# Normalising a softmax: sums and reciprocals moved through DRAM instead of through TensorE products

## The chip, the cores and the metric

The kernel runs on one core of a Trainium2 chip. The time is device microseconds of one launch, and the time before is the median of three runs, 3791.74 us (3791.0 to 3793.28). A profile of one execution stands beside it; its span is 3780.8 us.

The engines are called PE (TensorE), ACT (ScalarE), DVE (VectorE), POOL (GpSimd) and SP (SyncE, which issues nearly all transfers here). PEld is PE's weight load, which runs beside its products.

## The reference

Four layers follow one another on x of shape (4, 128, 64, 64): four images b, 128 channels, N = 4096 positions.

- Layer 0 is self-attention over positions: energy = q^T k with 16-dimensional q and k, `softmax(energy, axis=-1)`, out = v attn^T, and then `gamma * out + x`.
- Layer 1 is two 3x3 convolutions with quantised weights and activations, batch norm and a residual.
- Layer 2 is a selective scan (Mamba): projections, a recurrence h = dA * h + dBx over the 4096 positions for 256 inner channels and 16 states, an output product, a group norm, silu and a residual.
- Layer 3 is self-attention again, with 64-dimensional q, k and v, an output product wo, and a residual.

What matters here is the softmax of layers 0 and 3. For each of the 4096 output positions the kernel needs the sum of 4096 exponentials, and the 128 channels of that position are divided by it.

## The kernel before, in words

**Stages.** There are eight attention stages in the order of the list `stages`: layer 0 of images 0, 1 and 2, then layer 3 of image 0, layer 0 of image 3, and layer 3 of images 1, 2 and 3. An attention stage goes over 16 blocks of CB = 256 output positions, and each block over four quarters of the 4096 keys. A quarter (index t) is eight energy products (L491), two exponentials of 128x1024 on ACT (L507), the products with v (L544), and the products with a block of ones (L554) that give the sums. The products with v and the sums of a block gather in one PSUM tile `us` of 128 x 2 x 256: half 0 holds the channels, half 1 the sums. The sums arrive as four partial sums, each laid on 32 partitions in turn (partitions 0, 32, 64 and 96 carry one each), because the keys are split over four row groups of PE.

**The end of a block pair (`parts` and `finish`).** After each block ACT evicts both halves (L580, in layer 0 times gamma, and L582). Two blocks make 512 columns, index c of 8. For these `finish` runs. Its first four products (L601) with the column `sel4` (ones at partitions 0, 32, 64, 96) add the four partial sums and turn the 512 sums into columns, 128 x 4. DVE takes their reciprocals (L610). Four more products (L614), with each reciprocal column spread as weights against the identity, lay the reciprocals along rows, the same on all 128 partitions. DVE multiplies (L622). In layer 0 the result is added to x in the padded image `xpad` (L627). In layer 3 it goes through the output product (L633) and the residual addition (L637) and is stored (L640).

**Beside it** run the convolutions (`convolutions`), the preparation of the scan (`preparation`), and the scan. The scan goes over 512 steps m (4 images x 8 column blocks x 16 states). A step is, on DVE, the product of ud with the first half of a broadcast tile `bc` (L981), the readout of the step before with the second half of its tile (L971), and two recurrences (L989). ACT computes the decays `da` (L954) and copies the last column (L964); POOL adds up the readouts (L1006). Each `bc` tile is a 512 KB broadcast load from DRAM (L941) with three buffers, so the load for step m waits for the readout of step m-3.

**Order.** Nothing reorders at run time. The class `Order` plans all engines: each chain of work is a generator that yields `op(engine, time, needs)`, with its estimated time; `lag` is the estimated time after which a transfer's data has landed. The chain with the smallest estimated start plus 0.15 us times its rank is placed next. `finish` has rank 0, the scans rank 3. The result is one fixed list of instructions on each engine. One PSUM bank (`gtile`) is shared by the convolutions, the scan's products and `finish`; `bank=True` asks for it and `release` gives it back. `port=True` marks DVE work that the planner keeps apart from POOL's. SP is one such list too: a transfer that waits holds up those behind it.

The heart of the old `finish`:

```python
nc.tensor.matmul(sc[:, k : k + 1], lhsT=ss[:, k * P : (k + 1) * P], rhs=sel4, ...)
...
nc.vector.reciprocal(r, sc[:, 0:4])
...
nc.tensor.matmul(sc[:, k * P : (k + 1) * P],
                 lhsT=r[:, k : k + 1].to_broadcast([P, P]), rhs=ident, ...)
...
nc.vector.tensor_mul(us, us, sc)
```

Of the kernel before, what the change touches and what calls it, by code (L numbers as in the profile page):

```python
# [8 lines left out]
F32 = mybir.dt.float32  # L9
# [6 lines left out]
AF = mybir.ActivationFunctionType  # L16
ALU = mybir.AluOpType
AX = mybir.AxisListType
PSUM = bass.MemoryType.PSUM

P = 128
W = 64
N = W * W
TB = 512
NTB = N // TB
# [11 lines left out]
CB = 256  # L37
# [8 lines left out]
class Order:  # L46
# [16 lines left out]
    @staticmethod  # L63
    def op(engine, time, *needs, bank=False, table=None, port=False, lag=0.0):
        return engine, time, needs, bank, table, port or engine == "POOL", lag
# [6 lines left out]
    def mark(self, *key):  # L72
        self.marks[key] = self.end

    def release(self):
        self.bank = self.end[0]
# [36 lines left out]
def img(ap):  # L113
    return ap.rearrange("p (a b) -> p a b", b=W)


def inner(t, c):
    return t[:, 1 + c * ROWS : 1 + (c + 1) * ROWS, 1 : 1 + W]
# [14 lines left out]
def conv_seq_kernel(ctx: ExitStack, tc: tile.TileContext, i: dict, out: bass.AP):  # L133
    nc = tc.nc
    B = out.shape[0]

    const = ctx.enter_context(tc.tile_pool(name="const", bufs=1))
    sml = ctx.enter_context(tc.tile_pool(name="sml", bufs=2))
    dram = ctx.enter_context(tc.tile_pool(name="dram", bufs=2, space=bass.MemoryType.DRAM))
# [3 lines left out]
    att = fast.enter_context(tc.tile_pool(name="att", bufs=2))  # L143
# [6 lines left out]
    def gtile(name):  # L150
        return ps_g.tile([P, TB], F32, tag="g", name=name)
# [14 lines left out]
    for c in range(NTB // 2):  # L166
# [3 lines left out]
            out=staged[0, c],  # L170
            in_=i["x"][0].rearrange("c (k r) w -> c k (r w)", r=ROWS)[:, 2 * c : 2 * c + 2],
# [3 lines left out]
    ident = const.tile([P, P], F32, tag="ident", name="ident")  # L175
# [44 lines left out]
    for key, d, t in (("i", 2 * D0, bq0r), ("j", D0, bk0r)):  # L220
        low = [const.tile([P, 1], F32, tag=k + key, name=k + key) for k in ("low_", "lowb_")]
        r = ident.rearrange("p (a k b) -> p k a b", k=2, b=d)
# [5 lines left out]
    gam0 = const.tile([P, 1], F32, tag="gam0", name="gam0")  # L228
    nc.scalar.dma_start(out=gam0, in_=i["L0_conv_gamma"].unsqueeze(0).to_broadcast([P, 1]))
    gbv0 = const.tile([P, 1], F32, tag="gbv0", name="gbv0")  # L230
    nc.vector.tensor_mul(gbv0, gam0, bv0)

    sel4 = const.tile([P, 1], F32, tag="sel4", name="sel4")
    nc.gpsimd.memset(sel4, 0.0)
    for k in range(4):
        nc.gpsimd.memset(sel4[32 * k : 32 * k + 1, :], 1.0)

    def rsqrt(r, var):

# [98 lines left out]
    order = Order()  # L338
    op, mark, release = order.op, order.mark, order.release
# [18 lines left out]
    NQ = NJ // 8  # L358
    NS = NCB * NQ
    its, jts, vts, es, ps, uss = {}, {}, {}, {}, {}, {}  # L360
# [204 lines left out]
    def parts():  # L565


        for s, (layer, b) in enumerate(stages):
            for c in range(NTB):
                k0 = s * NCB + 2 * c  # L570
                us = ss = None
                for k in range(k0, k0 + 2):
                    need = [("parts", s * NTB + c - 2)] if s or c > 1 else []
                    yield op("ACT", 0.45, ("sums", (k + 1) * NQ - 1), *need)
                    if us is None:
                        us = att.tile([P, TB], F32, tag="us", name="us", bufs=2)
                        ss = att.tile([P, TB], F32, tag="ss", name="ss", bufs=2)
                    cols = slice((k - k0) * CB, (k - k0 + 1) * CB)
                    scale = gam0 if layer == 0 else 1.0
                    nc.scalar.activation(us[:, cols], uss[k][:, 0, :], AF.Copy, scale=scale)  # L580
                    yield op("ACT", 0.4)
                    nc.scalar.copy(ss[:, cols], uss.pop(k)[:, 1, :])  # L582
                    mark("evict", k)
                if layer == 3:
                    order.add(1, residual(b, c))
                order.add(0, finish(s, c, us, ss))

    def residual(b, c):
        n = NTB * b + c
        yield op("SP", 0.1, *([("out", n - 1)] if n else []), lag=2.5)  # L590
        outs[b, c] = o = att.tile([P, TB], F32, tag="o", name="o", bufs=1)
        nc.sync.dma_start(out=o, in_=x2s[b][c])
        mark("res", n)

    def finish(s, c, us, ss):
        layer, b = stages[s]
        n = 2 * NTB * b + (0 if layer == 0 else NTB) + c
        yield op("PE", 0.65, bank=True)
        sc = gtile("sc")
        for k in range(4):  # L600
            nc.tensor.matmul(  # L601
                sc[:, k : k + 1],
                lhsT=ss[:, k * P : (k + 1) * P],
                rhs=sel4,
                start=True,
                stop=True,
            )
        yield op("DVE", 0.18)
        r = rall[:, 4 * n : 4 * n + 4]
        nc.vector.reciprocal(r, sc[:, 0:4])  # L610

        yield op("PE", 1.15)
        for k in range(4):
            nc.tensor.matmul(  # L614
                sc[:, k * P : (k + 1) * P],
                lhsT=r[:, k : k + 1].to_broadcast([P, P]),
                rhs=ident,
                start=True,
                stop=True,
            )  # L620
        yield op("DVE", 0.69)
        nc.vector.tensor_mul(us, us, sc)  # L622
        release()
        if layer == 0:
            yield op("DVE", 0.75, ("x", b, c), port=True)
            xi = inner(xpad, c)
            nc.vector.scalar_tensor_tensor(xi, img(us), gbv0, xi, ALU.add, ALU.add)  # L627
            mark("xi", b, c)
            mark("parts", s * NTB + c)
        else:  # L630
            yield op("PE", 1.06, bank=True)
            g = gtile("o3")
            nc.tensor.matmul(g, lhsT=wo3, rhs=us, start=True, stop=True)  # L633
            mark("parts", s * NTB + c)
            yield op("DVE", 0.69, ("res", NTB * b + c))
            o = outs.pop((b, c))
            nc.vector.tensor_add(o, g, o)  # L637
            release()
            yield op("SP", 0.1, lag=2.5)
            nc.sync.dma_start(  # L640
                out=out[b].rearrange("c h w -> c (h w)")[:, c * TB : (c + 1) * TB], in_=o
            )
            mark("out", NTB * b + c)
# [369 lines left out]
    with tc.manual_schedule():  # L1013
        for rank, chain in (
            (1, parts()),
            (1, convolutions()),
            (1, preparation()),
            (1, output()),
            (1, lasts()),
            (3, energies()),  # L1020
            (4, exponentials()),
            (4, products()),
            (3, decays(0)),
            (3, decays(1)),
            (3, scans()),
            (3, additions()),
            (3, fetches()),
            (3, images()),
        ):
            order.add(rank, chain)  # L1030
        order.run()
# [9 lines left out]
    g = gtile("ok_t")  # L1041
# [470 lines left out]
```

## Time and profile before

| engine | busy us | share of the span | costliest lines |
|---|---|---|---|
| PE | 3462.1 | 92% | L544 1537.2, L491 530.2 + 195.5, L554 544.1 |
| DVE | 2963.8 | 78% | L989 1102.9 + 150.3, L971 669.2, L981 656.6 |
| ACT | 2512.8 | 66% | L507 1002.4, L954 702.0 |
| POOL | 1316.0 | 35% | L1006 1216.6 |

The groups of the change: L601 73.1 us and L614 73.2 us of PE (512 records each), L610 11.5 us and L622 43.8 us of DVE (64 each), L580 30.2 + 24.5 us and L582 46.8 us of ACT (128 each in all).

A share of the whole span mixes stages that have different limits. The page's row of 40 slices, each 94.5 us long, shows busy tenths per slice and tells the stages apart. A list of waits says, for each pair of lines, how long an engine sat idle until the other line ended, how often, and the longest such wait; "issue" means that nothing in the profile was waited for. A DMA row gives the number of transfers, the size of each and the median time from issue to landing. SPq in a timeline is SP issuing a transfer.

### The profile page before, as it was taken

How to read it: one execution, taken by the hardware profiler on the slowest of the kernel's cores; microseconds unless marked ns; L12 is line 12 of the kernel's file. 1: busy time of each engine (PE TensorE's matmuls, PEld its weight loads, DVE VectorE, ACT ScalarE, POOL GpSimd, SP SyncE). 2: the span in 40 equal slices, each digit the busy share in tenths (PEclk: the TensorE clock that was granted, in tenths of full speed). 3: DMA queues.
4: the chain of work that ended last, by engine and by line, in shares of the span. 5: the costliest groups of instructions: out<-in, count | busy, mean ns of one | idle time of the engine just before them, and what ended most of it. 6: DMA issues, size and time to landing. Idle time of an engine off the chain costs nothing.

```text
span 3780.8 us, 72475 instructions
## 1 busy us (share of the span) xinstructions
PE 3462.1 (92%) x30839; PEld 2258.3 (60%) x30839; DVE 2963.8 (78%) x2824; ACT 2512.8 (66%) x3658; POOL 1316.0 (35%) x568
## 2 busy tenths in 40 slices
PE   5999988999989999889998999999898988999998
PEld 3766656666656666645555666665454555556665
DVE  2039999999989999999998999989998888960000
ACT  2357767777776767677777777776776677764443
POOL 0004434444424444434443443443444444430000
PEclk8999999999999999999999999999999999999999
DMA  2013333333433333433443333333433433331000
GB/s 69 1 38 95 92 110 99 86 97 93 111 100 91 93 91 98 116 93 95 109 121 109 97 90 80 96 106 86 120 99 97 123 92 104 102 89 36 15 13 16
DMA packets 203662, 327.92 MB, mean 87 GB/s; under 512 B 50608, under 2 KB 53440, under 8 KB 203328
## 3 DMA queue, kind: packets, MB, share of 16 engines
q1 hardware_dynamic: 196384, 322.09, 31.8%
q8 instruction: 243, 3.98, 0.4%
q10 hardware_dynamic: 6944, 1.10, 0.2%
q14 instruction: 91, 0.75, 0.1%
HBM read 304.27 MB, written 18.87 MB: 85 GB/s over the span
## 4 chain that ended last, share of the span: by engine, by line
PE 60%; DVE 23%; ACT 11%; issue 5%; DMA 2%; ACTq 0%; DVEq 0%; SPq 0%
PE us L544 24%; PE e L491 13%; DVE hs L989 9%; PE us L554 8%; DVE hs L981 4%; DVE hs L971 3%; ACT da L954 2%; ACT p L507 2%; PE conv L649 2%; PE xh L738 2%; PE sc L614 1%; PE proj L462 1%; PE proj L420 1%; PE yo L868 1%; PE sc L601 1%
## 5 line engine op out<-in xcount | busy, mean ns | idle before, releaser
L1006 POOL TENSOR_TENSOR y<-y,hs 128x1024 f32<-128x1024 f32 x512 | 1216.6, 2376 | 2050.1 <-DVE hs L971 2022.7
L544 PE MATMUL us<-p,v 128*32 128x256 f32 (+1 forms) x12288 | 1537.2, 390 | 125.0 <-ACT p L507 125.0
L544 PEld LDWEIGHTS us<-p,v 128*32 128x32 f32 (+1 forms) x12288 | 1009.6, 138 | 564.8 <-issue 171.6
L507 ACT ACTIVATE p<-e 128x1024 f32<-128x1024 f32 x1024 | 1002.4, 1019 | 430.3 <-PE e L491 258.5
L989 DVE TENSOR_TENSOR_SCAN hs<-da,hlast,hs 128x512 f32<-128x512 f32 x896 | 1102.9, 1264 | 40.8 <-ACT da L954 40.5
L954 ACT ACTIVATE da<-dt,amat 128x512 f32<-128x512 f32 x1024 | 702.0, 691 | 271.1 <-DVE hs L989 263.7
L971 DVE TENSOR_TENSOR hs<-hs,bc 128x1024 f32<-128x1024 f32 x512 | 669.2, 1307 | 40.1 <-ACT hlast L964 39.6
L981 DVE TENSOR_TENSOR hs<-ud,bc 128x1024 f32<-128x1024 f32 x512 | 656.6, 1282 | 0.2
L554 PE MATMUL us<-p,ones 128*32 128x256 f32 x8192 | 544.1, 383 | 0.0
L491 PE MATMUL e<-it,v 64*128 64x256 f32 x4096 | 530.2, 398 | 14.0 <-ACT p L507 12.5
L491 PEld LDWEIGHTS e<-it,v 64*128 64x128 f32 x4096 | 382.2, 191 | 162.2 <-issue 89.7
L610 DVE RECIPROCAL rall<-sc 128x4 f32<-128x4 f32 x64 | 11.5, 179 | 529.2 <-PE sc L601 529.2
L554 PEld LDWEIGHTS us<-p,ones 128*32 128x32 f32 x8192 | 236.6, 110 | 209.1 <-issue 67.7
L491 PEld LDWEIGHTS e<-it,j 64*128 64x128 f32 x2048 | 140.9, 189 | 102.9 <-issue 69.5
L491 PE MATMUL e<-it,j 64*128 64x256 f32 x2048 | 195.5, 309 | 6.9 <-ACT p L507 5.9
L964 ACT COPY hlast<-hs 128x2 f32<-128x2 f32 x448 | 85.6, 191 | 130.8 <-DVE hs L989 125.0
L989 DVE TENSOR_TENSOR_SCAN hs<-da,hs 128x512 f32<-128x512 f32 x128 | 150.3, 1206 | 1.8 <-ACT da L954 1.7
L738 PEld LDWEIGHTS <-w 128*128 128x128 bf16 x576 | 51.7, 98 | 106.5 <-issue 58.4
L738 PE MATMUL xh<-x,w 128*128 128x512 fp8e4 x384 | 94.6, 383 | 3.8 <-DVE x L709 2.8
L1010 POOL TENSOR_TENSOR y<-y,sz 128x1024 f32<-128x1024 f32 x32 | 95.8, 2995 | 2.5
L601 PEld LDWEIGHTS sc<-sel,ss 128*128 128x128 f32 x512 | 65.0, 190 | 40.2 <-issue 18.3
L601 PE MATMUL sc<-sel,ss 128*128 128x1 f32 x512 | 73.1, 254 | 14.5 <-ACT ss L582 10.4
(158 smaller groups left out, 2517.9 us busy)
## 6 DMA issues: line engine op xcount, KB each, us to landing
bc<-bc_d SPq DMA_DIRECT2D x512, 512.0 KB, 4.8
x_in<-in_x SPq DMA_DIRECT2D x16, 512.0 KB, 4.7
xpad<-in_x SPq DMA_DIRECT2D x32, 256.0 KB, 3.2
x_d<-yo SPq DMA_DIRECT2D x32, 256.0 KB, 2.5
x_in<-x_d SPq DMA_DIRECT2D x16, 512.0 KB, 6.1
o<-x_d SPq DMA_DIRECT2D x32, 256.0 KB, 5.3
out<-o SPq DMA_DIRECT2D x32, 256.0 KB, 2.7
bc_d<-xd SPq DMA_DIRECT2D x64, 32.0 KB, 1.7
```

The costliest lines, as they stand in the source:

```text
L491: nc.tensor.matmul(e[k % 4 // 2][:, k % 2, k // 4, :], lhsT=jts[s][row : row + D3, col : col + P], rhs=its[s][row : row + D3, c * CB : (c ...
L507: nc.scalar.activation(p, es[t][h], AF.Exp)
L544: nc.tensor.matmul(us[rows, 0, :], lhsT=vts[s][:, 8 * q + k, cols], rhs=ps[t, h][:, k % 2, k // 4, :], start=False, stop=False,)
L554: nc.tensor.matmul(us[32 * m : 32 * m + 32, 1, :], lhsT=ones[:, 0:32], rhs=ps[t, m // 2][:, k % 2, k // 4, :], start=False, stop=q == NQ - ...
L601: nc.tensor.matmul(sc[:, k : k + 1], lhsT=ss[:, k * P : (k + 1) * P], rhs=sel4, start=True, stop=True,)
L738: nc.tensor.matmul(g, lhsT=w3[:, k // len(rhs), lhs[k % len(rhs)] : lhs[k % len(rhs)] + P], rhs=x[:, rhs[k % len(rhs)]], start=(k == 0), s ...
L954: nc.scalar.activation(da, live["in", g][0][:, h, :], AF.Exp, scale=amat[:, h, n : n + 1])
L971: nc.vector.tensor_mul(hs, hs, bcs.pop(m)[:, 1:2, :].to_broadcast([P, 2, TB]))
L981: nc.vector.tensor_mul(hs, ud, bcs[m][:, 0:1, :].to_broadcast([P, 2, TB]))
L989: nc.vector.tensor_tensor_scan(hs[:, h, :], das.pop((m, h)), hs[:, h, :], hlast[:, n, h : h + 1] if g % NTB else 0.0, ALU.mult, ALU.add,)
L1006: nc.gpsimd.tensor_tensor(y, y, hss.pop(m), ALU.add)
L1010: nc.gpsimd.tensor_tensor(y, y, live.pop(("sz", g)), ALU.mult)
```

## The change

The eight products of `finish` are replaced by transfers. The four rows of partial sums (partitions 0, 32, 64, 96 of half 1 of `us`) are written to DRAM (`s_d`, 4 x 512). They are read back as `st`, 128 x 4 x 4, so that a partition holds four sums in four parts each. DVE adds the parts (`tensor_reduce`) and takes the reciprocals. These are written to DRAM (`r_d`, 512) and read back as `rb`, the same row on all 128 partitions. DVE multiplies by `rb` from SBUF, with gamma in the same instruction in layer 0. The two halves of a PSUM block are evicted by one copy instead of two, and `sel4` goes. The aim is to take this work off PE, the busiest engine.

```diff
-                    nc.scalar.activation(us[:, cols], uss[k][:, 0, :], AF.Copy, scale=scale)
-                    yield op("ACT", 0.4)
-                    nc.scalar.copy(ss[:, cols], uss.pop(k)[:, 1, :])
+                        us = att.tile([P, 2, 2, CB], F32, tag="us", name="us", bufs=2)
+                    nc.scalar.copy(us[:, :, k - k0, :], uss.pop(k))
...
-        yield op("PE", 0.65, bank=True)
-        sc = gtile("sc")
-        for k in range(4):
-            nc.tensor.matmul(
-                sc[:, k : k + 1],
-                lhsT=ss[:, k * P : (k + 1) * P],
-                rhs=sel4,
...
-        yield op("DVE", 0.18)
+        yield op("SP", 0.1, lag=2.2)
+        s_d = dram.tile([4, TB], F32, tag="s_d", name="s_d")
+        nc.sync.dma_start(out=s_d, in_=us[0:P:32, 1, :])
+        us = us[:, 0, :]
+        mark("s_d", k)
+        yield op("SP", 0.1, ("s_d", k), lag=2.5)
+        st = att.tile([P, 4, 4], F32, tag="st", name="st", bufs=2)
+        nc.sync.dma_start(out=st, in_=s_d.rearrange("g (p e) -> p g e", e=4))
+        mark("st", k)
+        yield op("DVE", 0.3, ("st", k))
         r = rall[:, 4 * n : 4 * n + 4]
-        nc.vector.reciprocal(r, sc[:, 0:4])
-
-        yield op("PE", 1.15)
-        for k in range(4):
-            nc.tensor.matmul(
-                sc[:, k * P : (k + 1) * P],
-                lhsT=r[:, k : k + 1].to_broadcast([P, P]),
-                rhs=ident,
...
-        yield op("DVE", 0.69)
-        nc.vector.tensor_mul(us, us, sc)
-        release()
+        nc.vector.tensor_reduce(r, st.rearrange("p g e -> p e g"), AX.X, ALU.add)
+        nc.vector.reciprocal(r, r)
+        yield op("SP", 0.1, lag=2.2)
+        r_d = dram.tile([TB], F32, tag="r_d", name="r_d")
+        nc.sync.dma_start(out=r_d.rearrange("(p e) -> p e", e=4), in_=r)
+        mark("r_d", k)
+        yield op("SP", 0.1, ("r_d", k), *([("mul", k - 1)] if k else []), lag=3.0)
+        rb = att.tile([P, TB], F32, tag="rb", name="rb", bufs=1)
+        nc.sync.dma_start(out=rb, in_=r_d.unsqueeze(0).to_broadcast([P, TB]))
+        mark("rb", k)
+        yield op("DVE", 0.75, ("rb", k), port=True)
+        scale = gam0 if layer == 0 else 1.0
+        nc.vector.scalar_tensor_tensor(us, us, scale, rb, ALU.mult, ALU.mult)
+        mark("mul", k)
```

## The prediction, made before the changed kernel had run

> **What bounds the kernel now.** First the page's slices of the span, to see which engine is full when:
>
> ```profile
> PE   5999988999989999889998999999898988999998
> DVE  2039999999989999999998999989998888960000
> ```
>
> There are three stages. Slices 1 to 3 are TensorE alone (attention of image 0 in layer 0). From slice 4 to 35 both rows stand at 8 or 9. After that DVE has nothing left and TensorE works through layer 3 of the last image. Next, busy time by stage (stretch, its length, then busy us and instructions of PE, weight loads, DVE, ACT, POOL, then clock and DMA):
>
> ```profile
> 252.00:3366.00 3114.00, 2859.93 (x24358) 1863.74 (x24360) 2902.04 (x2667) 2245.85 (x3342) 1308.95 (x543) 0.97 0.37 99
> 3500.00:3600.00 100.00, 99.45 (x1328) 62.44 (x1324) 3.12 (x6) 41.56 (x50) 0.00 (x0) 1.00 0.04 12
> ```
>
> 252 to 3366 us is the stretch of the scans. DVE is busy for 93.2% of it, PE for 91.8%: two engines share the bound, DVE slightly ahead. In the tail PE is at 99%. So PE time saved counts fully in the tail, and in the scan stretch only where it shortens a DVE wait. What DVE waits for, 300 to 3366 us:
>
> ```profile
> DVE rall L610 <- PE sc L601: 59.6, 37, 3.3
> DVE hs L989 <- ACT da L954: 42.2, 33, 6.9
> DVE hs L971 <- ACT hlast L964: 39.6, 39, 2.6
> DVE us L622 <- PE sc L614: 16.2, 23, 2.9
> ```
>
> L610 and L622 are the two waits which the change removes: 75.8 us. DVE never waits for the loads of bc. Now the end of the scan stretch, in the timeline of the SP queue and of the rest:
>
> ```profile
> 3386.95 5.42 SPq L932 DMA_DIRECT2D x_d<-yo  x8
> 3417.27 3.51 SPq L375 DMA_DIRECT2D x_in<-x_d  x4
> ```
>
> The last image is stored by 3392.4, plus 2.5 us to landing (the page's x_d row): 3394.9. Its load is issued only at 3417.3, when PE has finished image 2 and freed the p buffers. PE therefore enters the tail 22.4 us late. One block's end in the tail:
>
> ```profile
> 3730.94 1.05 PE L601 MATMUL sc<-sel,ss 128*128 128x1 f32 x8
> 3732.27 1.16 PE L614 MATMUL sc<-ident,rall 128*128 128x128 f32 x8 [0.28 <-DVE rall L610]
> 3733.36 2.00 PE L491 MATMUL e<-it,v 64*128 64x256 f32 x16
> ```
>
> From the first sum product to the next energies PE spends 3733.36 - 3730.94 = 2.42 us. Last, the landing times, page and two narrow windows of the DMA view:
>
> ```profile
> bc<-bc_d SPq DMA_DIRECT2D x512, 512.0 KB, 4.8
> xpad<-in_x SPq DMA_DIRECT2D x32, 256.0 KB, 3.2
> bc_d<-xd SPq DMA_DIRECT2D x64, 32.0 KB, 1.7
> ...
> bc_d<-xd SPq DMA_DIRECT2D x2, 32.0 KB, 4.3
> ...
> bc_d<-xd SPq DMA_DIRECT2D x2, 32.0 KB, 1.5
> ```
>
> The 4.3 us write was issued at 317.3, right behind a bc load; the 1.5 us one at 768.7, 4.4 us after one. A small write right behind a 512 KB load costs some 2.5 us more.
>
> **What the Trainium skill says.** "DMA: Bandwidth & Descriptors", section Queues, rings and completion order: what SP issues goes onto one row of rings, and each engine takes descriptors in ring order. The trace agrees: 4.3 against 1.5 us. [...] "SBUF — State Buffer", section SBUF: two separate sides: VectorE with two SBUF inputs and GpSimd reading SBUF exclude each other for a whole instruction. L627, of that kind, has 0.73 us at its least and 0.90 on average here: in agreement.
>
> **The change part by part.** The chain runs 64 times: 51 in the scan stretch (L610 has 51 instructions there), 3 before and 10 after, eight of these in the tail.
>
> *Removed on PE:* 2.42 us each. In the scan stretch 51 x 2.42 = 123 us of PE, which lie beside DVE work and count only through waits. In the tail seven blocks count, 7 x 2.42 = 16.9; the eighth is the last chain.
>
> *Evictions:* four ScalarE copies (L580 0.47 or 0.38, L582 0.37, twice) become two 128x512 reads of PSUM. L873 is such a read: 0.58. That saves 0.34 to 0.52 us per chain, about 27 us of ACT. ACT is at 72% in the scan stretch, so this too is felt only through waits for it.
>
> *DVE work:* away go 0.18 (L610) and 0.69 (L622). New are a sum over four columns, bounded by L610 and by the one-row maximum of L279 (0.27), taken at 0.25; a reciprocal, 0.17; and a multiply with both inputs in SBUF, 0.73 to 0.90 by L627, taken at 0.80. 1.22 - 0.86 = +0.36 us, 51 times: +18 us on the path.
>
> *Four transfers in a row, all on SP.* s_d and r_d are small writes: 1.8. st gathers 512 pieces of 16 bytes; xpad's load has 1024 pieces of 256 bytes and lands in 3.2, so st lies between 1.8 and 3.2, taken at 2.6. rb is half a bc load, between 3.2 and 4.8, taken at 3.4. Unloaded the four are 9.6 us; each small write behind a bc load adds 2.5.
>
> *Where DVE meets them.* I read the changed program's order with the DVE durations of the profile. The multiply stands on average 5.9 us of DVE work behind the reciprocal; r_d and rb need 1.8 + 3.4 + 0.4 for handing on = 5.6. But 12 of the 52 chains beside scans have 3.8 us or less. These are short by about 30 us together: the lower bound of the new waits. In 35 of 53 chains the sum stands directly behind L971's counterpart, which releases the next bc load, so r_d is issued about 0.4 us behind that load. Charging these 2.3 us, the shortfalls add up to about 94 us; if s_d is delayed as often and nothing overlaps, 75 more: 170 is the upper bound. Who is behind a blocked SP: bc loads, issued at one L971 and needed about 7 us later against 4.8 us to landing, which leaves some 2.2 us. SP itself is held at s_d until ACT's eviction and at r_d until DVE's reciprocal. Behind a late multiply stand the scans on DVE, for which ACT's decays wait, and in layer 3 PE's output product. I take the middle, 100 us (2 us per chain).
>
> *Others' waits:* L989 and L971 above, and 15 us for activations of the convolutions and statistics in the same list, are 97 us in all; with PE 123 us and ACT 27 us lighter I guess that a good third goes, 35 us.
>
> *Sum for DVE:* -75.8 + 100 + 18 - 35 = +7 us, so the last image is there at 3402 instead of 3394.9. In the changed order PE has no energies of image 2 left behind the last yo product; before there are eight groups. So PE is no longer late: the tail starts 3417.3 - 3402 = 15 us earlier.
>
> *Tail:* 16.9 saved. The last chain is longer: now 3.65 us from the end of the last sums (3767.98) to the output product (3771.63); then 0.6 + 9.6 + 0.4 + 0.8 + 0.5 for handing on = 11.9, +8.2. Net -8.7. The first scan also waits for such a chain, but the three chains before it save 3 x 2.4: about nothing.
>
> Total -15 - 9 = -24 us: 3791.7 - 24 = **3768 us**.
>
> **Rivals.**
> (a) *The transfers are hidden:* the order leaves room that idle time lengthens; for it speaks that DVE never waits for bc today. New waits 30 us: DVE -75.8 + 30 + 18 - 35 = -63, PE's lag goes as well: -22 - 63 - 9 = -94, 3698 us. Against it: SP's waits couple it to ACT and DVE four times per chain.
> (b) *The transfers become the wait:* both small writes are caught behind bc loads, or SP's waits hold up bc itself, so each chain costs DVE 4 us: 204 us, without relief on ACT 180. DVE +123 to +146; -22 - 9 on the other side: +92 to +115 us, but idle DVE lets other waits shrink, so some +70, 3862 us: slower. For it speaks the collision above; against it the order, which mostly leaves the unloaded time.
> (c) *A wash:* waits of 120 us, 3788.
>
> **How the numbers follow.** Forecast 0.42, (a) 0.20, (b) 0.27, (c) 0.11. The forecast's case reaches past no change with 0.05 of its chance. Faster 0.57, same 0.11, slower 0.32. The range, 3690 to 3848, takes in (a) and most of the way to (b).
>
> **What would show it.** Right: L601 and L614 gone, the waits of DVE for st and rb near 100 us in the scan stretch, r_d landing in about 4 us in most chains, the tail's blocks 2.4 us shorter, no PE lag before the last image's load. Wrong: DVE waits for st and rb under 50 us or over 150, DVE waiting for bc, or the last scan ending more than 50 us off 3366.

## The result, and the profile after

The changed kernel takes 4109.41 us (median of four runs, 4098.61 to 4112.26) against 3792.51 for the kernel before beside it: a ratio of 1.083, 95% interval 1.081 to 1.085. The forecast was 3768. The profiled execution has a span of 4106.2 us, 325.4 more than before.

First the page's slices of the kernel after, as they were read for the kernel before; each is 102.7 us long:

```profile
PE   5888988988888899888788899988788888847777
DVE  2039888888998998988787988889788788940000
PEclk8999999999999999999899999999899999968888
```

The stages are the same, but neither engine is full any more. In the scan stretch the nines have become eights; in the last four slices, where PE was at 9, it now stands at 7, at a lower granted clock. The kernel has turned from one bound by two engines into one that waits. By stage (stretch, length, busy us and instructions of PE, weight loads, DVE, ACT, POOL, then clock and DMA), for the scan stretch and for 100 us of the tail:

```profile
277.00:3632.00 3355.00, 2875.39 (x24117) 1826.62 (x24120) 2903.55 (x2720) 2248.24 (x3252) 1306.50 (x542) 0.93 0.40 97
3800.00:3900.00 100.00, 77.35 (x984) 46.35 (x980) 3.48 (x8) 31.32 (x35) 0.00 (x0) 0.88 0.07 17
```

DVE's work in the scan stretch is as it was (2903.55 against 2902.04 us), but the stretch is some 250 us longer. The loss splits by the starts of the first and the last scan: the first starts at 277 instead of 260.7 us (+16), from it to the last one it is 3354 instead of 3101 (+253), from there to the end 475 instead of 419 (+56). Together 325. These cuts lie at DVE's scans. When the scans end, PE still has attention of image 2 to do in the kernel before, and none in the kernel after, so the last part looks better than it is. A fairer cut is the last group of PE's projections of the last image (L462 before, L457 after), behind which both kernels have the same work left. It starts at 3440.3 and at 3676.4 us: 236 us are lost up to there and 89 behind it.

**Where DVE loses it.** The waits of DVE in the scan stretch, kernel after:

```profile
DVE rall L602 <- DMA st<-s_d: 194.2, 50, 8.3
DVE us L614 <- DMA rb<-r_d: 89.0, 39, 5.7
DVE hs L981 <- ACT da L946: 62.7, 32, 10.2
DVE hs L963 <- ACT hlast L956: 43.0, 38, 4.9
```

The two waits for PE (75.8 us) are gone, and 283.2 us for `st` and `rb` stand in their place. The scans' own two waits are 105.7 instead of 81.8. So -75.8 + 283.2 + 23.9 + 8.6 of added work (DVE was busy 2894.9 us between the same two scans before) = +240 of the +253.

**Where PE loses it.** The chain that ended last, followed through the end of one block pair in the tail of the kernel after (start, duration, what):

```profile
3823.99 0.91 PE us L549 x16
...
3824.92 0.59 ACT us L572
...
3825.53 1.68 DMA s_d<-us
...
3827.23 1.90 DMA st<-s_d
...
3829.15 0.19 DVE rall L602
...
3829.57 1.42 DMA r_d<-rall
...
3831.00 4.19 DMA rb<-r_d
...
3835.29 0.70 DVE us L614
...
3836.03 2.08 PE o L625 x2
3838.11 2.63 PE e L486 x16
```

The whole new chain lies on the path. PE finishes the pair's last sums (L549), and the next thing in its list is this same pair's output product (L625). It can't start before the multiply, so PE sits idle while four transfers run, though the next energies (L486) need nothing of them. This happens at every one of the eight pairs, though the last has no next energies; waits of PE in the tail:

```profile
PE o L625 <- DVE us L614: 91.3, 8, 11.6
```

And when PE resumes it is slow: in the timeline the two output products take 2.08 us here and 1.12 before, the next 16 energies 2.71 instead of 2.00. From this eviction to the next pair's (at 3876.51) it is 51.6 us. Before, a pair takes 40.96 us, as two of its output products show:

```profile
3694.32 1.13 PE L633 MATMUL o<-us,wo 128*128 128x512 f32 x2
3735.28 1.12 PE L633 MATMUL o<-us,wo 128*128 128x512 f32 x2
```

**Why the product stands there.** The engines' lists are written by the planner, and the planner thinks that the chain is done earlier than it can be. The old chain's first step was on PE. The new one's is on SP and names no need:

```python
    def add(self, rank, chain):
        ...
            self.chains.append([rank, chain, (0.0, None), first])
...
        yield op("SP", 0.1, lag=2.2)
```

A chain that is added begins at time 0.0; the start of its first step is the later of that and the clock of its engine. PE is the fullest engine and its clock in the plan should never be far behind, so for the old chain the missing need should do no harm (a run below puts it in). SP's can be: after its last transfer it has nothing planned, and its clock stays. The plan then lets `s_d` leave before the sums exist, and all that follows, DVE's sum and multiply and PE's output product, is planned too early by as much. On the chip SP then waits for the eviction; over the whole span, kernel after:

```profile
SPq L593 <- ACT us L572: 643.6, 50, 81.4
```

That wait alone decides nothing: in the first run below, where the plan knows of the eviction, it is still 500.4 us, 81.8 at most, since in some stages SP has little else to do. More telling is the room that the plan left: between a pair's second eviction (L572) and the sum (L602) DVE has on average 1.6 us of work, counted in the trace over the 53 chains between the first and the last scan, while `s_d` and `st` took 1.68 + 1.90 us in the tail, with no scans beside them. That is the theory which the experiments test. Its rival is the prediction's own rival (b): the transfers take longer beside the loads of the scans than the plan's lags of 2.2, 2.5, 2.2 and 3.0 us (9.9 in all) allow.

### The profile page after: what moved, and what is told of

The parts are those of the page before. It is cut to its first block, busy times and chain, and to the rows that moved or that the text cites. A ratio compares the mean times of both kernels' runs of the same rounds, so it can differ in the third digit from the quotient of the medians.

```text
span 4106.2 us, 70733 instructions
## 1 busy us (share of the span) xinstructions
PE 3436.6 (84%) x29810; PEld 2184.2 (53%) x29815; DVE 2972.3 (72%) x2888; ACT 2499.9 (61%) x3527; POOL 1314.9 (32%) x563
## 4 chain that ended last, share of the span: by engine, by line
PE 46%; DVE 24%; DMA 16%; ACT 8%; issue 5%; POOL 0%; ACTq 0%; SPq 0%; DVEq 0%; POOLq 0%
PE us L539 18%; PE e L486 11%; DVE hs L981 10%; PE us L549 7%; DMA rb<-r_d 5%; DVE hs L973 4%; DVE hs L963 4%; DMA st<-s_d 3%; DMA s_d<-us 3%; DMA r_d<-rall 3%; PE conv L641 2%; ACT da L946 2%; ACT p L502 1%; PE xh L730 1%; PE o L625 1%
## 5 line engine op out<-in xcount | busy, mean ns | idle before, releaser
L486 PE MATMUL e<-it,v 64*128 64x256 f32 x4096 | 558.8, 415 | 22.3 <-ACT p L502 21.4
L549 PE MATMUL us<-p,ones 128*32 128x256 f32 x8192 | 545.6, 384 | 0.0
L602 DVE TENSOR_REDUCE rall<-st 128x4 f32<-128x16 f32 x64 | 11.5, 180 | 692.6 <-DMA st<-s_d 692.6
L486 PEld LDWEIGHTS e<-it,v 64*128 64x128 f32 x4096 | 402.7, 201 | 195.3 <-issue 115.2
L549 PEld LDWEIGHTS us<-p,ones 128*32 128x32 f32 x8192 | 236.1, 110 | 218.8 <-issue 79.4
L486 PE MATMUL e<-it,j 64*128 64x256 f32 x2048 | 199.7, 311 | 20.2 <-ACT p L502 18.6
L486 PEld LDWEIGHTS e<-it,j 64*128 64x128 f32 x2048 | 142.2, 189 | 121.5 <-issue 69.1
L625 PE MATMUL o<-us,wo 128*128 128x512 f32 x64 | 49.5, 865 | 142.8 <-DVE us L614 126.6
L572 ACT COPY us<-us 128x512 f32<-128x512 f32 x128 | 74.8, 584 | 104.2 <-PE us L549 103.8
L641 PE MATMUL conv<-xh,wint 128*128 128x512 f32 x224 | 72.2, 468 | 52.5 <-ACT xh L663 45.5
```

The source lines that it names most:

```text
L486: nc.tensor.matmul(e[k % 4 // 2][:, k % 2, k // 4, :], lhsT=jts[s][row : row + D3, col : col + P], rhs=its[s][row : row + D3, c * CB : (c ...
L549: nc.tensor.matmul(us[32 * m : 32 * m + 32, 1, :], lhsT=ones[:, 0:32], rhs=ps[t, m // 2][:, k % 2, k // 4, :], start=False, stop=q == NQ - ...
L641: nc.tensor.matmul(img(g), lhsT=wt[:, n, :], rhs=src[:, c * ROWS + dy : (c + 1) * ROWS + dy, dx : dx + W], start=start and n == 0, stop=st ...
```

## The experiments

Each ratio is to the kernel before, run beside it.

**The need alone.** One edit to the kernel after, which tells the plan when the data exist:

```diff
-        yield op("SP", 0.1, lag=2.2)
+        yield op("SP", 0.1, ("evict", s * NCB + 2 * c + 1), lag=2.2)
```

> One edit of the changed kernel: the first transfer of each chain (s_d) is planned no earlier than the eviction that makes its data. Theory 1 (planning): the chain's first step carries no need, so the planner starts it at SP's clock, before the eviction, and puts the sum, the multiply and the output product up to tens of us too early in the lists of DVE and PE; with the need the tail's blocks go from about 51 us back to under 42, DVE's waits for st and rb in the scan stretch from 280 to under 120 us, and the time to 3740 to 3830 us. Theory 2 (transport): the four transfers themselves, behind bc loads, are too slow for the planned lags; then the waits for st and rb stay above 200 us in the scan stretch and the time above 3950 us.

3857.96 us, ratio 1.0182 (1.016 to 1.0204). Not one instruction is another; only their order is. It gives back nearly four fifths of the loss, in both stages: first to last scan 3206 us instead of 3354, tail 384 instead of 475. Waits of DVE in its scan stretch:

```profile
DVE us L614 <- DMA rb<-r_d: 86.6, 44, 5.8
DVE rall L602 <- DMA st<-s_d: 73.1, 35, 7.7
```

The wait for `st`, in the half of the chain that starts at the missing need, falls from 194.2 to 73.1; DVE now has 4.6 us of work between the eviction and the sum. The one for `rb` stays: its half starts at DVE's reciprocal and was planned from there all along. So the time lies between the two forecasts, and what is left has another cause. The need also mends a third place: before the first scan PE waits 20.0 us in the kernel after, in two waits of a convolution (L641) whose image a chain had still to finish. Both waits are gone here, and the first scan starts at 265.8 instead of 277.1 us.

**The lags alone.** Kernel after, no need, each planned lag 2.0 us longer:

```diff
-        yield op("SP", 0.1, lag=2.2)
+        yield op("SP", 0.1, lag=4.2)
...
-        yield op("SP", 0.1, ("s_d", k), lag=2.5)
+        yield op("SP", 0.1, ("s_d", k), lag=4.5)
...
-        yield op("SP", 0.1, lag=2.2)
+        yield op("SP", 0.1, lag=4.2)
...
-        yield op("SP", 0.1, ("r_d", k), *([("mul", k - 1)] if k else []), lag=3.0)
+        yield op("SP", 0.1, ("r_d", k), *([("mul", k - 1)] if k else []), lag=5.0)
```

> One edit of the changed kernel: each of the four lags is 2 us longer in the plan (4.2, 4.5, 4.2, 5.0), the missing need is left missing. Theory 1: in the scan stretch SP's clock in the plan is never more than some 5 us behind, so 8 us more make up for most of it there, while in the tail, where SP is idle for 40 us per block, the output product stays right behind the sums and the blocks stay at about 51 us: 3850 to 3950 us. Theory 2: the lags are the whole trouble, so the tail's blocks shorten too and the time falls under 3830 us.

3871.0 us, ratio 1.0213 (1.0193 to 1.0234). In the scan stretch the 8 us make up for the missing need as well (waits of DVE for `st` 12.4, for `rb` 9.1 us; 3124 us from first to last scan). In the tail they do nothing. Waits of PE there:

```profile
PE o L625 <- DVE us L614: 90.8, 8, 11.5
```

There SP has done nothing since it stored the pair before (in the kernel after issued at 3838.87, with the next pair's eviction some 38 us later), and no lag of a few us reaches that far. So the two causes overlap beside the scans, and only the need mends the tail.

**The need in the last stage only.**

```diff
-        yield op("SP", 0.1, lag=2.2)
+        last = s == len(stages) - 1
+        yield op("SP", 0.1, *([("evict", s * NCB + 2 * c + 1)] if last else []), lag=2.2)
```

> The changed kernel with the need on the eviction in the last attention stage alone (the tail). It splits the loss. Theory 1: the tail's eight blocks give back about 10 us each, 4010 to 4045 us, and the scan stretch stays as slow as in the changed kernel. Theory 2: the tail keeps its blocks of about 51 us and the time stays within 15 us of 4109.

3994.45 us, ratio 1.0541 (1.0518 to 1.0564), a little below the expected range. The tail is 378 us instead of 475, the scan stretch nearly unchanged (3337; waits for `st` and `rb` 188.3 and 82.4). Of eight waits of PE one is left, that of the last chain, which has nothing to hide behind:

```profile
PE o L626 <- DVE us L615: 11.1, 1, 11.1
```

**Both.** The need and the longer lags together:

> Both edits together: the need on the eviction, and lags 2 us longer each. The scan stretch of the run with long lags (3125 us from first to last scan) and the tail of the run with the need (some 384 us behind the last scan) fit together as 266 + 3125 + 384 = 3775 us of span. Theory 1 and 2 joined (the plan started the chain too early AND its lags were too short for a loaded queue): 3755 to 3800 us, waits of DVE for st and rb in the scan stretch under 40 us. If transfers cost something that no plan hides, for instance SP's queue holding up bc, it stays above 3830 us.

3774.25 us, ratio 0.9968 (0.9956 to 0.9979): 0.3% faster than the kernel before. The order is now right in the tail; timeline of a pair's end there in this kernel:

```profile
3673.71 0.59 ACT L572 COPY us<-us 128x512 f32<-128x512 f32 x1 [1.18 <-PE us L549]
3674.32 0.50 SPq L593 DMA_DIRECT2D s_d<-us  x1
...
3683.80 0.69 DVE L614 SCALAR_TENSOR_TENSOR us<-us,rb 128x512 f32<-128x512 f32 x1 [5.50 <-DMA rb<-r_d]
...
3692.52 0.59 ACT L572 COPY us<-us 128x512 f32<-128x512 f32 x1 [1.18 <-PE us L549]
3694.31 1.12 PE L625 MATMUL o<-us,wo 128*128 128x512 f32 x2
```

The chain takes about as long as in the kernel after (3674.32 to 3684.49, 10.2 us; there 10.5), but the output product comes a block later, at 3694.31, behind the next eviction. PE waits for nothing and is back at 1.12 us for the two products. Its windows, scan stretch and tail:

```profile
277.00:3390.00 3113.00, 2790.11 (x23937) 1778.14 (x23936) 2919.16 (x2713) 2236.86 (x3240) 1321.85 (x542) 0.96 0.41 104
3600.00:3700.00 100.00, 100.00 (x1342) 61.26 (x1334) 5.22 (x12) 41.70 (x45) 0.00 (x0) 1.00 0.10 25
```

PE is full again in the tail. A pair takes 3694.31 - 3655.63 = 38.68 us, 2.28 less than before. DVE's waits in the scan stretch:

```profile
DVE hs L963 <- ACT hlast L956: 57.3, 49, 5.0
DVE hs L981 <- ACT da L946: 55.0, 34, 7.9
...
DVE rall L602 <- DMA st<-s_d: 7.4, 5, 3.4
```

The transfers are hidden (the row for `rb` has 2.7 us), but the scans wait 112.3 us for ACT, where it was 81.8 before. First to last scan is 3116 us, not below the 3101 of before, and the stretch behind it is 383 against 419. This does not say that the whole gain is in the tail: once more PE has no attention of image 2 left at that point and instead waits 21.7 us for POOL's last readouts. The last groups of projections, before and here:

```profile
3440.29 2.00 PE L462 MATMUL proj<-L_conv_wvT,x_in 128*128 128x64 f32 x16
3437.17 2.00 PE L457 MATMUL proj<-L_conv_wvT,x_in 128*128 128x64 f32 x16
```

PE gets there 3.1 us earlier, and from there to the end it is 334.9 instead of 340.5 us. So 3.1 us of the 8.7 between the two profiled executions come before that point and 5.6 behind it. In the first control below (a planned eviction of 0.46 us), which keeps the eight products, the stretch behind the last scan is 386 us too, with 340.5 us from this point to the end.

**The need and lags near what the loaded transfers showed** (3.2, 3.2, 3.6, 4.2):

> As the run before, with lags nearer to the landing times that the traces show beside scans (3.2, 3.2, 3.6, 4.2 in place of 2.2, 2.5, 2.2, 3.0). Between the need alone (3858) and need with long lags: 3750 to 3830 us. If shorter lags are better than the long ones, since a chain planned too long delays layer 0's images and the eviction of the next pair, it is the fastest of all.

3779.23 us, ratio 0.998 (0.9971 to 0.9989). The lags planned for slow transfers do no worse than those planned for the mean, and probably a little better; the two intervals overlap slightly.

**The last chain by the eight products.** The kernel with both edits, and the very last pair ends in the old way:

```diff
+        if k == len(stages) * NTB - 1:
+            us, ss = us[:, 0, :], us[:, 1, :]
+            yield op("PE", 0.65, ("evict", s * NCB + 2 * c + 1), bank=True)
...
+            yield op("DVE", 0.69)
+            nc.vector.tensor_mul(us, us, sc)
+            release()
```

> The run with need and long lags, but the very last chain of the kernel goes by the eight products again. That chain has nothing beside it: it took 11.8 us from the last sums to the output product by transfers there, and 3.65 us in the kernel before. Theory 1 (what is left is only latency without cover): 8 us less than need and long lags, 3762 to 3770 us, and below the kernel before by 0.4 to 0.7%. If the end is set by something else, no change: 3774.

3762.52 us, ratio 0.9921 (0.9907 to 0.9935), 12 us less than with both edits alone. From the end of the last sums to the output product it is now 3.6 us, with the transfers it was 11.2; to the end of the span 12.7 instead of 23.2, since PE is also slow after that wait. This is the best complete version found, 27 us under the kernel before.

**The single eviction alone.** The kernel before, with its products kept, but with one eviction of 128x512, and gamma moved into the multiply:

```diff
-                    nc.scalar.activation(us[:, cols], uss[k][:, 0, :], AF.Copy, scale=scale)
-                    yield op("ACT", 0.4)
-                    nc.scalar.copy(ss[:, cols], uss.pop(k)[:, 1, :])
+                    nc.scalar.copy(us[:, :, k - k0, :], uss.pop(k))
...
-        nc.vector.tensor_mul(us, us, sc)
+        scale = gam0 if layer == 0 else 1.0
+        nc.vector.scalar_tensor_tensor(us, us, scale, sc, ALU.mult, ALU.mult)
```

> The kernel before with one part of the change alone: one eviction of both halves of a block, gamma in the multiply; the eight products stay. Theory 1 and 2 alike: this part is harmless, 27 us less of ACT off the path, 3760 to 3800 us. A third theory, that the single eviction of 0.58 us or the layout of us is to blame, would put it above 3850 us.

3807.84 us, ratio 1.0057 (1.0035 to 1.008): a lighter ACT and a slower kernel. Waits of DVE for ACT's `da` and `hlast` are 106.0 us, 24 more than before, in the same two rows that are high in the kernel with both edits. Two controls ask whether any disturbance of the plan does this: a planned eviction of 0.46 instead of 0.45 us, and the need put on the old chain's first product.

> A control: the kernel before with the planned time of one ACT eviction 0.46 instead of 0.45 us. No instruction is added or taken away, only the order that the planner finds. It measures how far the planner's choice alone moves the time: I expect 3770 to 3815 us, so that the 22 us which the single eviction alone cost lie within it. If it stays within 5 us of the kernel before, the single eviction has a cost of its own.

> The kernel before with the same need on the eviction put on its first product. There the chain's first step is on PE, whose clock in the plan is never far behind, so theory 1 says that the missing need does little harm there: 3760 to 3815 us. If the need is worth 100 us or more here as well, it is not the move to SP that made it matter.

3784.98 us, ratio 0.9994 (0.9985 to 1.0003), and 3792.63 us, 1.001 (1.0002 to 1.0017). So a changed plan alone is worth about 0.1% in these two, not 0.57%. The second also shows that the old chain did not lack the need. The cost thus seems to be the single eviction's own, but why one is worse than two stays open. The multiply with gamma is not it (45.9 us in all against 43.8), and the time is lost before the last projections (3463.5 against 3440.3).

**Half of the transfers.** The sums become columns by the four products again, and only the reciprocals travel. Its reciprocals land at other columns than their sums came from.

```diff
+        yield op("PE", 0.65, ("evict", s * NCB + 2 * c + 1), bank=True)
+        sc = gtile("sc")
+        for q in range(4):
+            nc.tensor.matmul(
+                sc[:, q : q + 1], lhsT=ss[:, q * P : (q + 1) * P], rhs=sel4, start=True, stop=True
+            )
...
+        nc.vector.reciprocal(r, sc[:, 0:4])
+        release()
+        yield op("SP", 0.1, lag=4.2)
```

> Half of the change: the columns of sums by the four products, the reciprocals along rows by transfers (r_d and rb, lags 4.2 and 5.0), the need on the eviction. PE gains 1.2 us less per chain, the chain is two transfers shorter. If PE's relief is what brings the gain, slower than with all four transfers by up to 20 us, 3775 to 3800; if waits for transfers still cost in the scan stretch, faster, 3750 to 3770.

3752.54 us, ratio 0.9896 (0.9878 to 0.9914). To put every reciprocal at its own column, the next kernel lets each product take every fourth column of sums; its instructions stand in the same order on PE, DVE and SP:

```diff
-                sc[:, q : q + 1], lhsT=ss[:, q * P : (q + 1) * P], rhs=sel4, start=True, stop=True
+                sc[:, q : q + 1], lhsT=cs[:, q], rhs=sel4, start=True, stop=True
```

Here `cs` is `us[:, 1, :].rearrange("p (c e) -> p e c", e=4)`.

> Half of the change again, with every fourth column in each product, so that the columns of reciprocals lie as r_d lays them along rows (in the run before they fell to the wrong positions: that kernel left the right placing out). The instructions are as many and of the same sizes, so the time should be that of the run before, 3745 to 3765 us; a weight load with a step of four could cost PE up to 0.2 us x 4 per chain.

3849.55 us, ratio 1.0144 (1.0127 to 1.0161): 97 us slower than the run before, and far above what was expected. Weight loads of this line (duration ns: least, median, most), contiguous columns first:

```profile
L600 PEld LDWEIGHTS sc<-sel,us x512: 186/192/338, 116.8 to 3730.5; 128*128 128x128 f32 x171
```

And with every fourth column:

```profile
L601 PEld LDWEIGHTS sc<-sel,us x512: 307/329/332, 117.5 to 3828.3; 128*128 128x128 f32 x171
```

A load with a step of 16 bytes takes 137 ns longer, 512 x 0.137 = 70 us in all. Each product also needs both evictions now, where two of the four could start after the first: idle time of the weight loads until an eviction is 49.0 us against 13.6. Which of the two makes how much of the 97 us was not separated. Writing `r_d` in pieces of 4 bytes instead was not tried. With the last chain by the eight products as well:

> As the run before, and the last chain by all eight products. The two remaining transfers of that chain (about 7 us from the reciprocals to the output product) have nothing beside them; products take 2 us: 4 to 6 us less, 3742 to 3758 us, below both kernels of the case.

3840.6 us, ratio 1.0126 (1.0109 to 1.0143): again some 9 us for the last chain, and above its expectation for the same reason.

## Why the prediction was wrong

**What failed.** Two steps: what was allowed for the transfers ahead of DVE's sum, and what was put at nothing in the tail.

*"Where DVE meets them".* The bounds of 30 and 170 us rest on the room between the reciprocal and the multiply. That half was read well: 30 to 94 us were given to it, and the wait for `rb` is 89.0. For the half ahead of the sum, `s_d` and `st`, no room was read; it got 75 us, as an upper bound and by analogy. 194.2 came. The need alone takes 121 us of that away, so most of it is the plan's early start. The sign of it was even seen ("In 35 of 53 chains the sum stands directly behind L971's counterpart"), and was read as a collision of `r_d` with a `bc` load. In the trace it is 41 of 53 in the kernel after, and with the need 14 of 52: it was the mark of a plan that starts the chain early. And only 23 of the 53 `r_d` were issued within 2 us of a `bc` load; from there to the issue of `rb` they took 3.62 us in the median, the others 1.92.

*"Tail: 16.9 saved".* The products removed were subtracted without a look at where the output product now stands in PE's list. That it stands behind a late multiply was named, but no cost was put on it. Seven waits of about 11.4 us that other work could have filled, a slow clock after each, and the longer last chain made the stretch behind the last projections 89 us longer, where 8.7 us less had been forecast.

Two of the prediction's signs of being wrong came: waits for `st` and `rb` over 150 us, and a last scan more than 50 us off 3366.

*Smaller misses.* The relief for "others' waits" of 35 us did not come: the scans' waits for ACT grew by 24 us in the kernel after, and by 30 in the one with both edits. And the first scan was taken as unmoved; it starts 16 us later. The need mends 11 of these; with the longer lags as well it is 13 us later than before, but only 6 later with the middle lags (266.4), so planning the chain longer seems to cost time there. *PE's lag before the last image* (22 us) vanished with both edits, as predicted, but brought little: the last image is also stored later, and PE reaches its last projections 3.1 us earlier, not 15. In the first control the lag is gone as well (from the last `x_d` store to the last load 6.2 us, before 28.4), with the eight products in place, so the transfers are not needed to remove it.

**What held.** *Two engines share the bound, and PE counts fully in the tail:* yes; 2.42 us for a pair was the forecast, 2.28 the measured gain once the order allows it. *The landings:* 9.6 us were predicted unloaded; 1.68 + 1.90 + 1.42 + 4.19 = 9.2 were measured, with `rb` undersized (3.4) and the small ones oversized. *The eviction:* 0.58 predicted, 0.584 measured. *DVE's work:* +18 predicted, +8.6 measured. *The last chain:* 8.2 us longer predicted, 11.2 against 3.65 measured.

*The collision on the SP queue* exists too. The Trainium skill ("DMA: Bandwidth & Descriptors", Queues, rings and completion order) has descriptors taken in ring order, and the trace agrees. The chain that ended last in the kernel after, beside scans:

```profile
2097.52 0.38 SPq L933
...
2097.99 6.14 DMA st<-s_d
...
2104.58 1.40 DMA r_d<-rall
...
2106.00 4.09 DMA rb<-r_d
```

`st` follows a `bc` load (L933) by half a microsecond and lands after 6.14 us, in the tail after 1.90. Rival (b), which had the right direction at 3862 us, named this collision as the cause. It did not foresee the missing need; but once the need is there, the kernel stands near it, at 3858 us, with 160 us of waits for `st` and `rb`. The collision is a part of these: in that trace 13 of 52 `s_d` and 14 of 52 `r_d` were issued within 2 us of a `bc` load, and took 3.67 and 4.11 us in the median until the transfer that reads them was issued, the others 1.83 and 2.19. The shares of the two causes depend on the order: the need first gives 251 us and the lags then 84, the lags first 238 and the need then 97. The rival's other half, that `bc` itself is held up, is hardly in the traces: DVE never waits for it in the kernel after, and 2.2 us with both edits.

**The sum.** In medians, from the kernel after: need in the last stage -115, in the other seven -136, lags -84, last chain -12: 4109 to 3762.5 us. With the need and the lags in, the design takes 3774 us, close to the 3768 forecast. That is in part chance: against the kernel before beside it the gain is 14 us of the 24, and the larger of the forecast's two terms, 15 us from an earlier start of the tail, came to 3.1. The forecast had priced the transfers and the work; what decided was when the plan believed them done.

## What to carry to other kernels

Where a plan fixes every engine's list, moving the first step of a chain to an engine that idles needs an explicit dependency on its data; an engine whose clock in the plan always kept up may have stood in for it. After such a change look, on each engine, at what now stands directly before and behind the consumers of the chain, and count the room from the moment the data exist. Work taken off a full engine pays only if its list has something else to do in the meantime. And a split of the time at one engine's last instruction moves with what the other engines still have to do; cut where the work left is the same.

## What the runs showed of the hardware

- After some 11 us without work PE came back slow: 2.08 us for two products that take 1.12 otherwise, 2.71 for 16 energies that take 2.00, and a granted clock of 0.88 in that tail where the kernel with both edits has 1.00. The Trainium skill ("TensorE: Matmul & The Clock Gate", Part 1: The HAM clock gate) has the array at half its clock after an idle window of about 3.4 us, until it has been busy as long. The trace agrees in that the products take nearly twice as long after the wait, and that the energies from 3843.59 on, 7.6 us after PE resumed, take 2.00 again; the length of the window is not shown here. Idling thus cost about 1.7 us more at each pair than the wait itself.
- An fp32 weight load with a column step of 16 bytes took 329 ns, a contiguous one 192. The Trainium skill ("SBUF — State Buffer", Door 1: The DMA port swizzle) speaks of 16-byte lines and of a penalty for each access that crosses to a new one; the trace shows a longer load, by 137 ns, as such a penalty would make it; no run here varies the step.
- A row of 2 KB read from DRAM onto all 128 partitions (256 KB) landed in 4.19 us, not much under the 4.8 of a broadcast of twice the size.
